# Attention with image prompts: the inputs turned by VectorE in squares of 32, the query weights in the order that this gives

## The chip, the cores and the metric

The kernel runs on one core of a Trainium2 chip. The metric is the device time of one execution in microseconds (us); the median of several executions counts. A core has five engines with a queue of instructions each: TensorE (PE in the profile; its weight loads are PEld), VectorE (DVE), ScalarE (ACT), GpSimd (POOL) and SyncE (SP). SyncE, ScalarE and GpSimd also issue DMA transfers. SBUF is the memory on the chip with 128 partitions; four quadrants of 32 partitions each play a part here. PSUM holds what TensorE writes, in eight banks.

## The reference

For a batch of 8, with 112 positions of 320 channels (`x`) and a context of 375 rows of 512 (`ctx`), of which the last 4 are image tokens, attention with 20 heads of 16 channels is computed twice, over the text and over the image tokens, and added:

```python
q = heads(x @ W_q)
k_t, v_t = heads(text @ W_k), heads(text @ W_v)          # text = ctx[:, :-4], 371 rows
probs_t = softmax(q @ k_t^T * 0.25)
text_out = probs_t @ v_t
k_ip, v_ip = heads(ip @ W_k_ip), heads(ip @ W_v_ip)      # ip = ctx[:, -4:]
qsem = l2norm(probs_t @ text)                            # 512 wide for every head and position
fused = q @ k_ip^T * 0.25 + 0.5 * (qsem @ l2norm(ip)^T)
probs_ip = softmax(fused) * spatial_mask
out = (text_out + probs_ip @ v_ip) @ W_out + b_out + x
```

## The kernel before, in words

**Steps.** The work goes in 40 steps (b, g): batch element b = 0 to 7, and group g = 0 to 4 of four heads. `qsem` is never formed. Instead the Gram matrix of a context, `ug`, is computed once for each batch element (`ps_g`, L460 for b = 0, else L498), doubled off its diagonal, with GpSimd halving the diagonal blocks (L482), and spread by SyncE's transfers to `u` (L512), four partition quadrants for the four heads of a group. The values of the text (`ps_v`, L567) go out to DRAM (L592) and come back as `vr` (L601), and GpSimd copies them beside the Gram matrix into `u` (L648). One large product for each step, `ps_qd<-u,xgT` (L730), then gives the norms of `qsem`, the text output and the products with the image tokens at a time. `xgT` are the turned probabilities of the step.

**One step.** TensorE forms the scores of four heads (`ps_s`, L682) from the keys `kT` and the queries `qm`; VectorE takes the row maxima (`nmx`, L695); ScalarE takes the exponentials (`p`, L699); SyncE moves them into four quadrants (`xg<-p`, L706); VectorE turns them in squares of 32 (`xgT`, L718); TensorE multiplies (L730); ScalarE takes the values out (`pvs`, L757) and VectorE reduces the rest (L783). Scores run two steps ahead of the product that uses them (`LEAD` = 2).

**Contexts.** The context of b = 0 is turned by TensorE against an identity matrix (`ps_c`, L430). The others are loaded in four quadrants (`load_ctx`) and turned by VectorE (`ctxT<-ct`, L418). With squares of 32, quadrant a of the result then holds channels of quadrant a of the load, so that the weights that meet this result must hold their rows in the same order; those of keys and values are loaded so.

**Queries.** Inputs are handled in five lots, `pairs` = [0], [1, 2], [3, 4], [5, 6], [7]. `x_sb` holds x by position (112 partitions), for the residual as well. `project_queries` turns a lot by identity products (`ps_x`, L332, three blocks of channels, one product for each batch element and block), each block into a PSUM bank of its own; ScalarE copies it to `xT` (L335), and nine products with `wq_sb` follow (`ps_q`, L361, and L343 for the narrow third block), whose results VectorE spreads to `qm` (L370, L353). In `xT` and `wq_sb` channel 128 i + p lies in block i, partition p; the third block is half zeros.

**What sets the order.** Nothing is scheduled by costs: the order of PE, DVE, SP, and in the steps of ACT and POOL too, is the order of the Python code, written by hand (`tc.manual_schedule`). The prologue starts everything for b = 0; then steps run in twos: `pair(n - 1)` or `alone(n)` multiplies two steps while scores of later ones are mixed in, and `behind(n)` puts the other work of a batch element (next keys `k`, values `v`, queries `q`, Gram matrix `gr`, finish `f`) behind the products. The next lot's queries are projected in `behind(n)` at even b and g = 2: its first place is the prologue (b = 0), the second b = 0, g = 2, then b = 2, 4 and 6.

**Banks.** Three pools hold the PSUM banks: `qd` (a ring of four), `sc` and `mm` (two each). `bank()` draws from the pool that the list `turn` names next; `turn` is set at the start of each `behind(n)`. A draw from a ring waits until the bank's former user has been read:

```python
elif b % 2 == 0 and g == 2:
    turn[:] = ["qd"] * 6 + ["mm"]
```

**The residual's input.** `load_inputs` (L310, GpSimd) fetches the remaining batch elements of x in three pieces, at steps n = 0 (in `behind`) and at n = 7 and 17 by the table `inputs`.

Of the kernel before, what the change touches and what calls it, by code (L numbers as in the profile page):

```python
# [8 lines left out]
F32 = mybir.dt.float32  # L9
# [11 lines left out]
def kernel(  # L21
# [81 lines left out]

    x_sb = const.tile([S, B, C], F32, tag="x_sb", name="x_sb")
    wq_sb = const.tile([P, NC, CP], F32, tag="wq_sb", name="wq_sb")
    wk_sb = const.tile([P, NE, C], F32, tag="wk_sb", name="wk_sb")
# [59 lines left out]
    ident = const.tile([P, P], F32, tag="ident", name="ident")  # L166
    make_identity(nc, ident)
    nc.gpsimd.memset(wq_sb[REST:, FULL, :], 0.0)

# [97 lines left out]
    def prompt_projections():  # L267
# [26 lines left out]
        for i in range(NC):  # L294
            nc.vector.tensor_tensor(
                kipb[:, i],
                kip[:, i, :NIP].unsqueeze(1).to_broadcast([P, HC, NIP]),
                hmask.unsqueeze(2).to_broadcast([P, HC, NIP]),
                ALU.mult,
            )  # L300
# [11 lines left out]
    queries = {}  # L312
    pairs = [[0]] + [list(range(b, min(b + 2, B))) for b in range(1, B, 2)]

    def project_queries(bs):
        n = len(bs)
        xT = work.tile([P, NC, 2 * S], F32, tag="xT", name=f"xT_{bs[0]}", bufs=1)
# [5 lines left out]
        nc.gpsimd.memset(xT[REST:, FULL, :], 0.0)  # L323
        for i in range(NC):
            cn = min(P, C - i * P)
            if bs[0] == 0:

                ps = ps_qd.tile([P, 512], F32, tag="qd", name=f"ps_x_0_{i}")
            else:
                ps = bank(f"ps_x_{bs[0]}_{i}", spare=bs[0] > 1 and i > 0)  # L330
            for j, b in enumerate(bs):
                nc.tensor.transpose(  # L332
                    ps[:cn, j * S : (j + 1) * S], x_sb[:, b, i * P : i * P + cn], ident[:S, :S]
                )
# [114 lines left out]
    def first_gram():  # L449

        ctxT = st[0]["ctxT"]
        banks = []
        for c in range(NT):
            banks.append(ps_qd.tile([P, 512], F32, tag="qd", name=f"ps_g_0_{c}"))
            if c == NT - 1:
                nc.gpsimd.tensor_copy(ctxT[:, :, TT:T], ipnT[:, :, :NIP])
            c0, c1 = c * P, min(c * P + P, T)
            for r in range(c + 1):
                for e in range(NE):
                    nc.tensor.matmul(  # L460
                        banks[r][:, c0 - r * P : c1 - r * P],
                        ctxT[:, e, r * P : (r + 1) * P],
                        ctxT[:, e, c0:c1],
                        start=(e == 0),
                        stop=(e == NE - 1),
                    )
                if c == NT - 1:
                    doubled(banks[r], r, 0)
                yield
# [585 lines left out]
    run(("q", 0), lambda: project_queries(pairs[0]), 3)  # L1055
# [3 lines left out]
    run(("q", 0), None)  # L1059
    run(("k", 0), lambda: keys(0))  # L1060
# [13 lines left out]
    placed(0, 0)  # L1074
    run(("k", 0), None, 2)
    more_constants()
    turn[:] = ["mm", "mm", "sc"]
# [52 lines left out]

    inputs = {7: (3, 5), 17: (5, B)}

    late = (1, 5)

    def pair(n):
# [40 lines left out]
        if g == 2:  # L1176
            turned(b + 2)
        value_sums(b, g)

        b, g = two  # L1180
# [32 lines left out]
    def behind(n):  # L1213
# [9 lines left out]
        if b % 2 == 0 and g == 0:  # L1223
            if n == 0:
                turn[:] = ["sc", "sc", "mm"]
            else:
                turn[:] = ["qd"] * 4 + ["mm"]
                k(b)
                nc.scalar.preload_act_table(AF.Sqrt)
                f(b - 1)  # L1230
                if b - 1 < B - 2:
                    prompt_values(b - 1)
# [13 lines left out]
            load_next(b + 2)  # L1246
            if n == 0:
                load_inputs(1, 3)
        elif b % 2 == 0 and g == 2:
            turn[:] = ["qd"] * 6 + ["mm"]  # L1250
            gram_to_groups(nb, (2,))
# [3 lines left out]
            else:  # L1255
                k(nb)
            q(nb, 3)
            tr(0)
# [55 lines left out]
        else:  # L1314
            turn[:] = ["qd"] * 3 + ["sc"]
            v(nb)
            f(b - 1)
# [9 lines left out]
    for n in range(0, len(steps) - NG, 2):  # L1327
# [145 lines left out]
```

## Time and profile before

| what | value |
| --- | --- |
| median of 3 runs | 413.02 us (412.82 to 413.89) |
| profiled execution | 412.12 us |
| its span, first to last instruction | 410.4 us |
| mean granted clock of TensorE | 0.998 |
| busy: PE, DVE, ACT, POOL | 98%, 81%, 47%, 28% of the span |
| largest shares of the chain that ended last | `ps_qd` L730 44%, `ps_v` L567 13%, `ps_k` L528 10% |

"Busy" is the time in which an engine has an instruction under way. Rows of the groups by line read: line, engine, operation, output<-input, number of instructions, then busy time and mean ns of one, then idle time before them and what ended it. Rows of a timeline read: start in us, duration in us, engine, line, operation, output<-input, number of instructions taken together, and in brackets the idle time of the engine ahead of them and what ended it. The queue that issues transfers has a q behind its engine (SPq, ACTq). The chain of waits follows the work that ended last back from instruction to instruction.

### The profile page before, as it was taken

How to read it: one execution, taken by the hardware profiler on the slowest of the kernel's cores; microseconds unless marked ns; L12 is line 12 of the kernel's file. 1: busy time of each engine (PE TensorE's matmuls, PEld its weight loads, DVE VectorE, ACT ScalarE, POOL GpSimd, SP SyncE). 2: the span in 40 equal slices, each digit the busy share in tenths (PEclk: the TensorE clock that was granted, in tenths of full speed). 3: DMA queues.
4: the chain of work that ended last, by engine and by line, in shares of the span. 5: the costliest groups of instructions: out<-in, count | busy, mean ns of one | idle time of the engine just before them, and what ended most of it. 6: DMA issues, size and time to landing. Idle time of an engine off the chain costs nothing.

```text
span 410.4 us, 14139 instructions
## 1 busy us (share of the span) xinstructions
PE 404.0 (98%) x5627; PEld 316.7 (77%) x5627; DVE 330.6 (81%) x700; ACT 194.8 (47%) x691; POOL 114.6 (28%) x271
## 2 busy tenths in 40 slices
PE   8999999999999999999999999999999999999996
PEld 8868687798777786878687877778777878687894
DVE  4356589877998887887999897887799997878985
ACT  3254342336443942524553664334733485346763
POOL 5103111121261352021161036002034125103681
PEclk9999999999999999999999999999999999999999
DMA  7777956988595746577666576576756444766311
GB/s 237 164 199 220 187 155 174 203 194 178 135 187 129 183 121 178 134 174 176 170 147 146 145 179 157 155 180 139 176 151 155 117 124 123 187 157 174 111 51 30
DMA packets 58245, 64.65 MB, mean 158 GB/s; under 512 B 19061, under 2 KB 52041, under 8 KB 58180
## 3 DMA queue, kind: packets, MB, share of 16 engines
q1 hardware_dynamic: 55230, 59.50, 59.4%
q10 hardware_dynamic: 2486, 2.69, 2.1%
q0 software_dynamic: 464, 1.56, 1.7%
q8 instruction: 45, 0.74, 0.8%
q14 instruction: 20, 0.16, 0.1%
HBM read 19.03 MB, written 5.22 MB: 59 GB/s over the span
## 4 chain that ended last, share of the span: by engine, by line
PE 93%; DMA 3%; POOL 2%; DVE 1%; ACT 0%; SPq 0%; issue 0%; POOLq 0%
PE ps_qd L730 44%; PE ps_v L567 13%; PE ps_k L528 10%; PE ps_g L498 7%; PE ps_s L682 7%; PE ps_o L886 3%; PE ps_k L545 3%; PE ps_q L361 3%; DMA u<-ug 2%; PE ps_g L460 1%; DMA xg<-p 1%; PE ps_w L447 1%; PE ps_c L430 1%; PE ps_q L343 1%; PE ps_o L982 0%; PE ps_a L877 0%
## 5 line engine op out<-in xcount | busy, mean ns | idle before, releaser
L730 PE MATMUL ps_qd<-u,xgT 32*112 32x40 f32 (+11 forms) x3840 | 215.8, 351 | 0.5 <-POOL u L648 0.4
L730 PEld LDWEIGHTS ps_qd<-u,xgT 32*112 32x112 f32 x3840 | 176.8, 172 | 36.1 <-issue 6.3
L718 DVE STREAM_TRANSPOSE xgT<-xg 128x768 f32<-128x768 f32 (+1 forms) x63 | 123.0, 1972 | 4.1 <-DMA xg<-p 3.9
L699 ACT ACTIVATE p<-ps_s,nmx 112x371 f32<-112x371 f32 x160 | 85.7, 586 | 58.2 <-DVE nmx L695 57.2
L695 DVE TENSOR_REDUCE nmx<-ps_s 112x1 f32<-112x371 f32 x160 | 77.1, 536 | 35.7 <-PE ps_s L682 33.7
L783 DVE CUSTOM_DVE_ANT_0 p<-ps_qd,p 112x371 f32<-112x371 f32 x152 | 73.5, 540 | 13.0 <-ACT pvs L757 8.3
L648 POOL COPY u<-vr 128x64 f32<-128x64 f32 x120 | 27.0, 237 | 199.0 <-PE ps_qd L730 116.4
L682 PE MATMUL ps_s<-kT,qm 32*112 32x375 f32 (+1 forms) x320 | 61.5, 485 | 0.0
L567 PE MATMUL ps_v<-wv_sb,ctxT 128*128 128x320 f32 x192 | 56.1, 439 | 0.3 <-ACT kT L535 0.3
L757 ACT COPY pvs<-ps_qd 112x21 f32<-112x21 f32 x152 | 21.9, 200 | 56.1 <-DVE ss L783 50.4
L567 PEld LDWEIGHTS ps_v<-wv_sb,ctxT 128*128 128x128 f32 x192 | 35.3, 190 | 14.6 <-ACT kT L535 1.0
L528 PE MATMUL ps_k<-ctxT,wk_sb 128*128 128x371 f32 x128 | 43.5, 483 | 0.0
L528 PEld LDWEIGHTS ps_k<-ctxT,wk_sb 128*128 128x128 f32 x128 | 23.1, 190 | 13.4 <-issue 1.3
L498 PE MATMUL ps_g<-ctxT 128*32 128x119 f32 (+11 forms) x672 | 32.4, 338 | 0.0
L498 PEld LDWEIGHTS ps_g<-ctxT 128*32 128x32 f32 x672 | 27.6, 109 | 6.0 <-issue 2.5
L682 PEld LDWEIGHTS ps_s<-kT,qm 32*112 32x112 f32 x320 | 27.7, 171 | 5.4 <-ACT p L699 0.4
L418 DVE STREAM_TRANSPOSE ctxT<-ct 128x512 f32<-128x512 f32 x21 | 22.5, 1082 | 6.0 <-DMA ct<-in_ctx_dram 6.0
L574 ACT COPY vext<-ps_v 128x320 f32<-128x320 f32 x24 | 10.2, 426 | 34.1 <-PE ps_v L567 25.5
L701 ACT COPY ipl<-ps_s 112x4 f32<-112x4 f32 x140 | 24.4, 174 | 0.0
L482 POOL TENSOR_TENSOR ug<-ug,half 128x128 f32<-128x128 f32 (+1 forms) x24 | 10.5, 447 | 32.9 <-ACT ug L481 28.1
L535 ACT COPY kT<-ps_k 128x371 f32<-128x371 f32 x16 | 7.5, 469 | 23.1 <-PE ps_k L528 22.8
L865 POOL TENSOR_TENSOR wv<-vip,w 112x1280 f32<-112x1280 f32 (+1 forms) x8 | 17.5, 2182 | 0.2 <-DVE w L859 0.2
(151 smaller groups left out, 317.6 us busy)
## 6 DMA issues: line engine op xcount, KB each, us to landing
xg<-p SPq DMA_DIRECT2D x159, 162.3 KB
u<-ug SPq DMA_DIRECT2D x128, 99.0 KB
ct<-in_ctx_dram SPq DMA_DIRECT2D x28, 176.0 KB
vip<-vipd SPq DMA_DIRECT2D x7, 560.0 KB
vr<-vd SPq DMA_DIRECT2D x20, 120.0 KB
out_dram<-ob SPq DMA_DIRECT2D x7, 140.0 KB
vd<-vext ACTq DMA_DIRECT2D x12, 80.0 KB
vr<-vd SPq DMA_DIRECT2D x12, 80.0 KB
```

Of the source, the lines that this page charges most:

```text
L418: nc.vector.transpose(ctxT[:, :, c * P : (c + 1) * P].rearrange("p e (j i) -> p j e i", i=RG), ct[:, some, :].rearrange("p j (k e) -> p j ...
L498: nc.tensor.matmul(ps[p * RG : (p + 1) * RG, s0 : T - t0], ctxT[:, e, t0 + q * RG : t0 + (q + 1) * RG], ctxT[:, e, t0 + s0 : T], start=(e ...
L528: nc.tensor.matmul(ps[:, :TT], wk_sb[:, e, i * P : (i + 1) * P], s["ctxT"][:, e, :TT], start=(e == 0), stop=(e == NE - 1),)
L567: nc.tensor.matmul(ps[:, :C], ctxT[:, e, c * P : (c + 1) * P], wv_sb[:, e, :], start=(e == 0), stop=(e == NE - 1),)
L648: nc.gpsimd.tensor_copy(region(b, c)[:, :, UV - c * P :], s["vr"][:, c * QN : (c + 1) * QN, g, :])
L682: nc.tensor.matmul(ps[:S, :w], qm[a * RG : (a + 1) * RG, i, r, j * S : (j + 1) * S], s["kT"][a * RG : (a + 1) * RG, i, :w], start=True, st ...
L695: nc.vector.tensor_reduce(nmx, ps[:S, :TT], AX.X, ALU.max, negate=True)
L699: nc.scalar.activation(p, ps[:S, :TT], AF.Exp, bias=nmx)
L701: nc.scalar.copy(s["ipl"][:, groups[g][a], :], ps[:S, TT:T])
L718: nc.vector.transpose(xT[:, j : j + n].rearrange("p j (k q) -> p q j k", q=QN), xg[:, :, j * RG : (j + n) * RG].rearrange("p q (j k) -> p ...
L730: nc.tensor.matmul(banks[a][:S, j * RG : UW], xT[a * RG : (a + 1) * RG, j, :S], region(b, c)[a * RG : (a + 1) * RG, p, q * RG :], start=(j ...
L783: nc.vector.tensor_tensor_reduce(out=p, in0=ps[:S, :TT], in1=p, scale=1.0, scalar=0.0, op0=ALU.mult, op1=ALU.add, accum_out=s["ss"][:, h : ...
```

## The change

x is loaded a second time in another form: `x_in` has 128 partitions, and quadrant q holds channels 80 q to 80 q + 79 of blocks of 32 positions, padded with zeros to 96. VectorE turns it in squares of 32 (`turned_inputs`, L353 of the changed kernel) straight to `xT`. Block i, quadrant q of `xT` then holds channels 80 q + 32 i onwards, so that `wq_sb` is loaded in that order: eight loads by GpSimd (L194, L198 of the changed kernel) in place of two by SyncE. The identity products L332, the copies L335 and the memsets L323 go. The product of a lot with its weights is as before. In `turn`, six draws from `qd` become three. The three small products of `kipb` (L295) go from VectorE to GpSimd. The residual's loads move to other steps, with batch element 0 among them.

```diff
-    nc.sync.dma_start(x_sb[:, 0, :], x[0])
-    load_channels(nc.sync, wq_sb, w_q)
...
+    def load_turned(eng, bs):
+        t0, n = blocks_of(bs)
+        rows = x.rearrange("b s c -> (b s) c")[t0 : t0 + n * RG, :]
+        for q in range(QN):
+            eng.dma_start(
+                x_in[q * RG : (q + 1) * RG, :n, :XW],
+                rows[:, q * XW : (q + 1) * XW].rearrange("(j i) c -> i j c", i=RG),
+            )
...
+    load_turned(nc.sync, pairs[0])
     load_embed(nc.sync, wk_sb, w_k)
     loaded[1] = load_ctx(1)
...
+    def load_query_weights(eng, quadrants):
+        for q in quadrants:
+            w = w_q[q * XW : (q + 1) * XW, :]
+            own = slice(q * RG, (q + 1) * RG)
+            eng.dma_start(
+                wq_sb[own, :FULL, :C], w[: FULL * RG, :].rearrange("(i c) f -> c i f", c=RG)
+            )
+            last = XW - FULL * RG
+            eng.dma_start(wq_sb[q * RG : q * RG + last, FULL, :C], w[FULL * RG :, :])
...
-            nc.vector.tensor_tensor(
+            nc.gpsimd.tensor_tensor(
                 kipb[:, i],
...
+    def turned_inputs(bs, i0=0, i1=NC):
...
+        nc.vector.transpose(
+            xT[:, i0:i1, : n * RG].rearrange("p i (j r) -> p j i r", r=RG),
+            x_in[:, :n, i0 * RG : i1 * RG].rearrange("p j (i c) -> p j i c", c=RG),
+        )
...
-        for i in range(NC):
-            cn = min(P, C - i * P)
-            if bs[0] == 0:
-                ps = ps_qd.tile([P, 512], F32, tag="qd", name=f"ps_x_0_{i}")
-            else:
-                ps = bank(f"ps_x_{bs[0]}_{i}", spare=bs[0] > 1 and i > 0)
-            for j, b in enumerate(bs):
-                nc.tensor.transpose(
-                    ps[:cn, j * S : (j + 1) * S], x_sb[:, b, i * P : i * P + cn], ident[:S, :S]
-                )
-            nc.scalar.copy(xT[:cn, i, : n * S], ps[:cn, : n * S])
-            yield
...
             if c == NT - 1:                                   # first_gram
                 nc.gpsimd.tensor_copy(ctxT[:, :, TT:T], ipnT[:, :, :NIP])
+                load_query_weights(nc.gpsimd, range(1, QN))
...
     awake(3)                                                  # prologue
+    load_query_weights(nc.gpsimd, range(1))
...
     order_values()
+    turned_inputs(pairs[0])
...
     placed(0, 0)
     run(("k", 0), None, 2)
+    load_turned(nc.gpsimd, pairs[1])
...
-    inputs = {7: (3, 5), 17: (5, B)}
+    inputs = {5: (0, 2), 9: (2, 5), 19: (5, B)}
...
         value_sums(b, g)                                      # pair
+        if b % 2 == 0 and b > 0 and g == 1:
+            turned_inputs(pairs[b // 2 + 1], 0, FULL)
...
                 turn[:] = ["sc", "sc", "mm"]                  # behind, n == 0
+                turned_inputs(pairs[1])
...
-            turn[:] = ["qd"] * 6 + ["mm"]
+            turn[:] = ["qd"] * 3 + ["mm"]
...
-            q(nb, 3)
             tr(0)
             v(nb)
             q(nb)
...
             turn[:] = ["qd"] * 3 + ["sc"]                     # behind, odd b, g == 3
+            load_turned(nc.gpsimd, pairs[(b + 3) // 2])
...
+        if b % 2 == 0 and b > 0 and g == 2:                   # main loop
+            turned_inputs(pairs[b // 2 + 1], FULL, NC)
         if n < len(steps) - NG - 1:
             value_sums(b, g)
             reduced(b, g)
```

**TensorE at the second place (b = 0, g = 2).** `ps_qd` are the last products of step (0, 2), `ps_v` the values of b = 1, `ps_q` its queries. The order before:

```order
L730 MATMUL ps_qd_2_1_704<-u_167,xgT_2_666 112x40
L290 MATMUL ps_kipT<-ident,kv 128x32 x3
L332 MATMUL ps_x_0_832<-ident,x_sb 128x112 x2
L332 MATMUL ps_x_1_836<-ident,x_sb 128x112 x2
L332 MATMUL ps_x_2_840<-ident,x_sb 64x112 x2
L567 MATMUL ps_v_1_846<-wv_sb,ctxT_246 128x320 x4
L361 MATMUL ps_q_0_852<-xT_829,wq_sb 128x224 x3
L567 MATMUL ps_v_2_862<-wv_sb,ctxT_246 128x320 x4
L730 MATMUL ps_qd_3_0_874<-u_167,xgT_3_844 112x392
```

And with the change:

```order
L761 MATMUL ps_qd_2_1_711<-u_170,xgT_2_673 112x40
L320 MATMUL ps_kipT<-ident,kv 128x32 x3
L598 MATMUL ps_v_1_838<-wv_sb,ctxT_259 128x320 x4
L391 MATMUL ps_q_0_845<-xT_589,wq_sb 128x224 x3
L598 MATMUL ps_v_2_855<-wv_sb,ctxT_259 128x320 x4
L761 MATMUL ps_qd_3_0_867<-u_170,xgT_3_836 112x392
```

The three rows of `ps_x` are gone, and the value product stands right behind the prompt's keys; the rest keeps its order.

**VectorE at the third place (b = 2).** `p_1` and `ss` are the reductions of step (2, 1), `nmx_4` the row maxima of step (2, 4), `p_2` the reductions of step (2, 2). The order before:

```order
L783 ISA ss_985 112x1
L695 TENSOR_REDUCE nmx_4_2_2142<-ps_s_2_2138 112x1
L695 TENSOR_REDUCE nmx_4_3_2148<-ps_s_3_2140 112x1
L695 TENSOR_REDUCE nmx_4_0_2169<-ps_s_0_2165 112x1
L695 TENSOR_REDUCE nmx_4_1_2174<-ps_s_1_2167 112x1
L783 ISA p_2_1822,ss_985<-ps_qd_2_0_2082,p_2_1822 112x371
```

And with the change:

```order
L814 ISA ss_978 112x1
L353 STREAM_TRANSPOSE xT_2120<-x_in 128x7x2x32
L726 TENSOR_REDUCE nmx_4_2_2142<-ps_s_2_2138 112x1
L726 TENSOR_REDUCE nmx_4_3_2148<-ps_s_3_2140 112x1
L726 TENSOR_REDUCE nmx_4_0_2169<-ps_s_0_2165 112x1
L726 TENSOR_REDUCE nmx_4_1_2174<-ps_s_1_2167 112x1
L353 STREAM_TRANSPOSE xT_2120<-x_in 128x224
L814 ISA p_2_1820,ss_978<-ps_qd_2_0_2080,p_2_1820 112x371
```

The lot is turned in two parts, 448 columns ahead of the four row maxima and 224 behind them, ahead of the next reductions.

**GpSimd in the prologue.** `ug` are the halvings of the first Gram matrix, `u` the values put beside it. The order before:

```order
L456 COPY ctxT_163<-ipnT 128x4x4
L482 TENSOR_TENSOR ug<-ug,half 128x128 x2
L482 TENSOR_TENSOR ug<-ug,half 128x115
L406 COPY ctxT_246<-ipnT 128x4x4
L323 MEMSET xT_278 64x224
L1058 COPY wq_sb<-wq_sb 128x3x64
L648 COPY u_167<-vr_168 128x4x16 x3
```

And with the change, from the last two of the eight loads of the query weights on:

```order
L194 DMA wq_sb<-in_L_xattn_W_q_dram 32x2x320
L198 DMA wq_sb<-in_L_xattn_W_q_dram 16x320
L513 TENSOR_TENSOR ug<-ug,half 128x128 x2
L513 TENSOR_TENSOR ug<-ug,half 128x115
L436 COPY ctxT_259<-ipnT 128x4x4
L1090 COPY wq_sb<-wq_sb 128x3x64
L679 COPY u_170<-vr_171 128x4x16 x3
L175 DMA x_in<-in_x_dram 32x7x80 x4
```

Two of the eight loads stand ahead of the copy of `ipnT` (L456 before) and six behind it, ahead of the halvings; four loads of the second lot of x stand behind the values.

More of the change, by code (lines that the diff above doesn't have):

```diff
@@ L104 @@
     x_sb = const.tile([S, B, C], F32, tag="x_sb", name="x_sb")
+    XW = C // QN
+    x_in = const.tile([P, 2 * S // RG, NC * RG], F32, tag="x_in", name="x_in")
     wq_sb = const.tile([P, NC, CP], F32, tag="wq_sb", name="wq_sb")
@@ L312 @@
     queries = {}
-    pairs = [[0]] + [list(range(b, min(b + 2, B))) for b in range(1, B, 2)]
+    inputs_turned = {}
+    def turned_inputs(bs, i0=0, i1=NC):
+        t0, n = blocks_of(bs)
+        if bs[0] not in inputs_turned:
+            inputs_turned[bs[0]] = work.tile(
+                [P, NC, 2 * S], F32, tag="xT", name=f"xT_{bs[0]}", bufs=1
+            )
+        xT = inputs_turned[bs[0]]
+        nc.vector.transpose(
+            xT[:, i0:i1, : n * RG].rearrange("p i (j r) -> p j i r", r=RG),
+            x_in[:, :n, i0 * RG : i1 * RG].rearrange("p j (i c) -> p j i c", c=RG),
+        )
     def project_queries(bs):
         n = len(bs)
-        xT = work.tile([P, NC, 2 * S], F32, tag="xT", name=f"xT_{bs[0]}", bufs=1)
+        at = bs[0] * S - blocks_of(bs)[0]
+        xT = inputs_turned.pop(bs[0])[:, :, at : at + n * S]
         qm = work.tile([P, NC, 2, 2 * S], F32, tag="qm", name=f"qm_{bs[0]}", bufs=2)
@@ L1058 @@
     nc.gpsimd.tensor_copy(wq_sb[:, :, C:], wq_sb[:, :, FULL * P : C])
-    run(("q", 0), None)
+    run(("q", 0), lambda: project_queries(pairs[0]))
     run(("k", 0), lambda: keys(0))
```

15 lines of the change are left out of this document (8 added, 7 removed).

## The prediction

> **What bounds the kernel now.** I read the page first, then the chain of waits, then the timeline of TensorE at the places where the change takes rows away, and last the timelines of VectorE, GpSimd and SyncE at the places where it puts rows in.
>
> From the page (span, busy time by engine, shares of the chain that ended last):
>
> ```profile
> span 410.4 us, 14139 instructions
> PE 404.0 (98%) x5627; PEld 316.7 (77%) x5627; DVE 330.6 (81%) x700; ACT 194.8 (47%) x691; POOL 114.6 (28%) x271
> PE 93%; DMA 3%; POOL 2%; DVE 1%; ACT 0%; SPq 0%; issue 0%; POOLq 0%
> ```
>
> TensorE is busy 98% of the span and is 93% of the chain: what leaves its queue leaves the time, unless what it waits for next is not ready earlier. VectorE, which receives the work, is busy 81%, so it has room only in definite gaps.
>
> **What TensorE loses.** All 24 turning products (L332) go, in five places. From the groups by line:
>
> ```profile
> L332 PE MATMUL ps_x<-ident,x_sb 112*128 112x112 f32 (+1 forms) x24 | 3.5, 264 | 0.1
> ```
>
> The 3.5 us are busy time, with neighbours overlapping. What a place costs is read between the start of its first turning product and the start of the value product behind it. From the chain of waits (start, us), the first and the fourth place, and from the timeline of TensorE the second, third and fifth:
>
> ```profile
> 15.88 0.29 PE ps_x L332 x3
> ...
> 252.94 0.58 PE ps_x L332 x6
> ```
>
> The other three:
>
> ```profile
> 59.02 1.21 PE L332 MATMUL ps_x<-ident,x_sb 112*128 112x112 f32 x6
> 60.29 2.42 PE L567 MATMUL ps_v<-wv_sb,ctxT 128*128 128x320 f32 x8
> ```
>
> ```profile
> 155.97 0.74 PE L332 MATMUL ps_x<-ident,x_sb 112*128 112x112 f32 x6
> 156.69 0.54 PE L567 MATMUL ps_v<-wv_sb,ctxT 128*128 128x320 f32 x1
> ```
>
> ```profile
> 349.58 0.45 PE L332 MATMUL ps_x<-ident,x_sb 112*128 112x112 f32 x3
> 350.30 0.54 PE L567 MATMUL ps_v<-wv_sb,ctxT 128*128 128x320 f32 x1 [0.27 <-ACT kT L535]
> ```
>
> Start to start that is 60.29 - 59.02 = 1.27, 156.69 - 155.97 = 0.72 and 350.30 - 349.58 = 0.72 us. Six products in a row are only 0.58 us of chain (the row at 252.94), so the rest of these gaps is a wait, and the change takes that away too. With six banks drawn from a ring of four, the value product gets the bank of the first draw and waits until ScalarE has emptied it. From the timeline of ScalarE:
>
> ```profile
> 59.94 0.29 ACT L293 COPY kip<-ps_kipT 128x96 f32<-128x96 f32 x1
> ```
>
> This ends at 60.23, 0.06 us before the value products start; in the last place the wait stands in the row at 350.30 itself, for a copy of ScalarE again (L535). After the change three banks are drawn, and the value product gets the second, which a score of the step before has left. The fourth place is built as the third, so I take 0.72 there as well (0.58 is the lower end). The sum on TensorE is 0.29 + 1.27 + 3 x 0.72 = 3.7 us; with the chain's 0.58, 0.58 and 0.53 (the copy in place of the products) for the last three it is 3.3.
>
> **What is late next at the second place.** The products behind it need the turned probabilities of their step (L718), on VectorE behind the three small products of L295. From the timelines of VectorE and TensorE:
>
> ```profile
> 61.76 0.39 DVE L295 TENSOR_TENSOR kipb<-kip,hmask 128x32 f32<-128x32 f32 x3
> 62.06 2.98 DVE L718 STREAM_TRANSPOSE xgT<-xg 128x1536 f32<-128x1536 f32 x1
> ```
>
> ```profile
> 65.93 0.60 PE L730 MATMUL ps_qd<-u,xgT 32*112 32x392 f32 x4
> ```
>
> TensorE would arrive at 65.93 - 1.27 = 64.66. L295 goes to GpSimd, so the turning starts at 61.76 and ends at 64.74: the step loses 0.1 us of its gain. On GpSimd the three products fall behind this row:
>
> ```profile
> 60.55 0.28 POOL L323 MEMSET xT<- 64x224 f32 x1
> 69.30 0.24 POOL L648 COPY u<-vr 128x64 f32<-128x64 f32 x1 [8.47 <-PE ps_qd L730]
> ```
>
> and the nearest product of two tensors on that engine is, in the groups,
>
> ```profile
> L482 POOL TENSOR_TENSOR ug<-ug,half 128x128 f32<-128x128 f32 (+1 forms) x24 | 10.5, 447 | 32.9 <-ACT ug L481 28.1
> ```
>
> No row shows them there. Three rows of 0.24 us (128 x 64, above) to 0.45 (L482, 128 x 128, below) would be 0.7 to 1.4 us of an idle 8.47, in which the memset L323 goes too: nothing, at both ends. They are first read by the prompt's logits, two steps later.
>
> **What VectorE gets.** Eight turnings, of 384 columns (the first place), 672 (second), 448 and 224 (third and fourth, each), 256 and 128 (fifth). Their price and the gaps they fall into, from the groups by form and the timeline of VectorE:
>
> ```profile
> L718 DVE STREAM_TRANSPOSE xgT<-xg 128x768 f32<-128x768 f32 x46 | 71.8, 1584 | 4.0 <-DMA xg<-p 3.9
> ```
>
> ```profile
> L418 DVE STREAM_TRANSPOSE ctxT<-ct 128x512 f32<-128x512 f32 x21 | 22.5, 1082 | 6.0 <-DMA ct<-in_ctx_dram 6.0
> ```
>
> ```profile
> 16.92 3.08 DVE L418 STREAM_TRANSPOSE ctxT<-ct 128x512 f32<-128x512 f32 x3 [6.00 <-DMA ct<-in_ctx_dram]
> ```
>
> ```profile
> 49.41 1.94 DVE L695 TENSOR_REDUCE nmx<-ps_s 112x1 f32<-112x371 f32 x4 [4.78 <-PE ps_s L682]
> ```
>
> ```profile
> 151.59 2.12 DVE L695 TENSOR_REDUCE nmx<-ps_s 112x1 f32<-112x371 f32 x4 [1.11 <-PE ps_s L682]
> ```
>
> ```profile
> 154.55 0.54 DVE L783 CUSTOM_DVE_ANT_0 p<-ps_qd,p 112x371 f32<-112x371 f32 x1 [0.84 <-ACT pvs L757]
> ```
>
> 1584 / 768 = 2.06 and 1082 / 512 = 2.11 ns a column; I take 2.11, since L418 has the same pattern of squares. So 0.81 us into a wait of 6.00, 1.42 into 4.78, 0.95 into 1.11, 0.47 into 0.84 (both twice), and 0.54 and 0.27 into the same two gaps of the last place. Together 5.9 us, all under cover by these rows, with 0.16 us to spare in the tightest; a gain is excluded, since VectorE only gets more to do. I cost them at nothing; uncovered, each costs what sticks out of its gap, on the way from the row maximum to the exponential and the transfer of the probabilities.
>
> **What the queues get.** SyncE issues four loads of x instead of three rows (x, and two of the query weights): one issue more, in a stretch where VectorE waits 6 us for the context. GpSimd now issues the query weights, eight loads, two before its copy at 8.49 and six behind it, ahead of the halving L482; then four loads of x for the second place ahead of more constants. The residual loads (L310) move: the one at 48.92 goes, the rest come later, with the first batch element added. From the view of that line, the timelines of GpSimd, SyncE and TensorE:
>
> ```profile
> L310 POOL DMA_DIRECT2D x_sb<-in_x_dram x3: 739/750/849, 48.9 to 208.4; - x3
> ```
>
> ```profile
> DMA to landing us min/median/max: 4.4/5.1/6.7
> ```
>
> ```profile
> 8.49 0.20 POOL L456 COPY ctxT<-ipnT 128x16 f32<-128x16 f32 x1 [2.51 <-DVE ipnT L262]
> 12.53 0.45 POOL L482 TENSOR_TENSOR ug<-ug,half 128x128 f32<-128x128 f32 x1 [3.84 <-ACT ug L477]
> ```
>
> ```profile
> 15.34 8.18 SPq L512 DMA_DIRECT2D u<-ug  x12
> ```
>
> ```profile
> 20.32 0.82 PE L361 MATMUL ps_q<-xT,wq_sb 128*128 128x112 f32 x6
> ```
>
> Six issues at 0.75 to 0.85 us from 8.69 on end at 13.2 to 13.8, so L482 starts 0.7 to 1.3 us later and its three rows end by 15.8 at worst, 0.5 us after SyncE asks for them at 15.34; those transfers are followed by ones that wait for the values anyway. The last weights are issued at 12.4 to 12.9 and land 4.4 to 6.7 us later, at 16.8 to 19.6; the first query product would now start at 20.32 - 0.29 = 20.03. So nothing is paid, with 0.4 us to spare at the far end.
>
> Here a rule of the skill speaks against the change. The Trainium skill, "SBUF — State Buffer", section "SBUF: two separate sides", says that GpSimd cannot write the descriptors of a load it issues while VectorE runs a copy in its two-port mode, and that the load should go to SyncE or ScalarE instead; the section behind it gives 3.1 us in place of 0.62 for one such load. The row that it would meet is this one, beside the second group of weight issues:
>
> ```profile
> 9.88 0.77 DVE L229 COPY wv_sb<-wv_in 128x512 f32<-128x512 f32 x2 [0.97 <-DMA wv_in<-in_L_xattn_W_v_dram]
> ```
>
> The rows of GpSimd above show no load issued beside these copies, so no run here shows it yet. If an issue waits out the 0.77 us of copies, the last weights come 0.8 us later, at 17.6 to 20.4, and TensorE waits at most 0.4 us. That is the second rival below, worked out from rows; by the skill's own figure the one load would be 2.5 us later and the sum 1 to 2 us smaller, an estimate from that page.
>
> At 86 us TensorE already waits for a transfer. From the timelines of GpSimd, TensorE and SyncE:
>
> ```profile
> 85.83 0.59 POOL L648 COPY u<-vr 128x64 f32<-128x64 f32 x3 [6.60 <-DMA xg<-p]
> ```
>
> ```profile
> 86.12 0.66 PE L730 MATMUL ps_qd<-u,xgT 32*112 32x392 f32 x3 [0.41 <-POOL u L648]
> ```
>
> ```profile
> 61.90 6.69 SPq L512 DMA_DIRECT2D u<-ug  x8
> ```
>
> ```profile
> 101.00 5.03 SPq L512 DMA_DIRECT2D u<-ug  x8
> ```
>
> If SyncE's chain of transfers before it did not move, the first two gains would end there. But the eight issues at 61.90 take 1.66 us longer than the eight at 101.00: I read the difference as a wait for the transfers of the values, which ScalarE issues when the value product is done; the trace does not name it. The value product moves 1.3 us earlier, so I expect the chain to move with it. The price of this wait lies between 0 (all moves) and 0.29 + 1.27 = 1.6 us (nothing moves); I take 0.3, near the lower end, by the 1.66 us that the row at 61.90 has over the one at 101.00.
>
> **The sum.** 3.7 - 0.1 - 0.3 = 3.3 us. The profiled execution took 412.12 us (410.4 of span and 1.7 around it), so 408.8 under the profiler; the median of the three runs is 413.02, 0.9 above, and with the same gain becomes 409.7.
>
> **The rivals.** (1) VectorE becomes the bound (slower). It is 81% busy, and two of the gaps are 1.11 us for 0.95: from 2.5 ns a column on (1.11 us over 448) the turnings stick out and delay the row maxima, the exponentials and the probabilities' transfers behind them. If all 5.9 us of them less the 0.39 of L295 came on the path, the time would be 413.0 - 3.6 + 5.5 = 414.9 (3.6 is the sum without the 0.1 of the second place). Against it stand 67 turnings in the two rows at 2.06 to 2.11 ns and the four waits quoted. The Trainium skill, "VectorE: DVE Perf Modes", section "Rules for kernel authors", advises TensorE for turning a 128 x 128 block where PSUM will do as the target; by that rule this rival would be the likelier one, and the waits quoted speak against it. Chance 0.10. (2) The query weights are late: at the far ends of issue and landing, with the copies waited out, the first query product waits 0.4 us, and twice that if the late halving also holds the first transfers: 3.3 - 0.8 = 2.5 saved, 410.5. Chance 0.10. (3) The transfers before 86 us don't move: 0.29 and 1.27 are lost in a longer wait there and 3 x 0.72 = 2.2 stays, 410.9; for it speaks that SyncE's eight issues from 61.90 on take 6.69 us already. Chance 0.17. (4) The change does nothing in the sum, (2) and (3) together with small waits in VectorE's gaps: 413.0. Chance 0.06. The forecast has the remaining 0.57; its own range is 2.8 us saved (3.3 by the chain, less 0.1 and the 0.4 of a doubled wait at 86) to 4.1 (3.7, and the 0.41 at 86 gone).
>
> **How the numbers follow.** No change here means within 0.3%, 1.24 us, about what a measurement of this kernel can tell: 411.8 to 414.3. Forecast, (2) and (3) are faster, 0.84, of which I leave 0.03 to each of the other two for sums of small waits not seen: faster 0.78, same 0.09 (rival 4 and these), slower 0.13 (rival 1 and these). The low end is 4.1 us saved and the 0.2 by which the quickest of the three runs, 412.82, lies under their median: 408.7. The high end is 412.0, halfway between (3) and (4), which leaves out (1), (4) and little else.
>
> **What would show it.** In the profile after, the value products at 15.7, 57.5, 154 and 251 us should follow their forerunners without the gap, the eight new turnings should be 2.1 ns a column with nmx (L695) starting as soon as before after its scores, and the wait at 86 should stay near 0.4 us. Wrong would be: a wait of TensorE for wq_sb near 20, a wait of 1.5 us or more where 86.12 was, or row maxima that start later behind their scores than before.

## The result, and the profile after

The changed kernel takes 411.23 us (median of 6 runs, 410.17 to 411.83) against 412.92 for the kernel before (6 runs): a ratio of 0.9959, 95% interval 0.9944 to 0.9974. It is faster, clear of the noise but by less than half a per cent: 1.7 us where 3.3 were forecast. The profiled execution took 411.26 us, 0.9 less than that of before.

The page after (span, busy time by engine, shares of the chain):

```profile
span 409.5 us, 14124 instructions
PE 402.0 (98%) x5603; PEld 316.1 (77%) x5603; DVE 333.5 (81%) x705; ACT 191.4 (47%) x676; POOL 127.6 (31%) x294
PE 92%; DMA 3%; SPq 2%; POOL 1%; ACT 1%; issue 0%; DVE 0%; POOLq 0%
```

TensorE is still the bound and has lost 2.0 us of work (404.0 to 402.0), but SyncE's queue is now on the chain with 2%. TensorE's timeline at the first, second and third place, first after, and then the one row of before that was not shown:

```profile
13.55 6.63 PE L598 MATMUL ps_v<-wv_sb,ctxT 128*128 128x320 f32 x24
```

```profile
61.12 0.35 PE L320 MATMUL ps_kipT<-ident,kv 32*128 32x32 f32 x3
61.40 2.42 PE L598 MATMUL ps_v<-wv_sb,ctxT 128*128 128x320 f32 x8
```

```profile
154.60 2.76 PE L559 MATMUL ps_k<-ctxT,wk_sb 128*128 128x371 f32 x8
157.20 2.05 PE L598 MATMUL ps_v<-wv_sb,ctxT 128*128 128x320 f32 x7
```

```profile
153.37 2.76 PE L528 MATMUL ps_k<-ctxT,wk_sb 128*128 128x371 f32 x8
```

The value products now follow their forerunners without a gap. From keys to values the third place takes 157.20 - 154.60 = 2.60 us; before it took 156.69 - 153.37 = 3.32. What was lost stands in the prologue. The waits of TensorE after:

```profile
PE ps_qd L761 <- POOL u L679: 1.1, 1, 1.1
PE ps_kv L304 <- DMA wip<-in_L_xattn_W_v_ip_dram: 0.4, 1, 0.4
```

TensorE's timeline there, before:

```profile
36.40 1.22 PE L730 MATMUL ps_qd<-u,xgT 32*112 32x392 f32 x10
...
41.76 2.42 PE L567 MATMUL ps_v<-wv_sb,ctxT 128*128 128x320 f32 x8
44.02 2.66 PE L528 MATMUL ps_k<-ctxT,wk_sb 128*128 128x371 f32 x8
46.60 1.29 PE L274 MATMUL ps_kv<-wip,ipT 128*32 128x160 f32 x32
47.83 1.22 PE L730 MATMUL ps_qd<-u,xgT 32*112 32x392 f32 x10
```

And after:

```profile
31.52 4.65 PE L529 MATMUL ps_g<-ctxT 128*32 128x375 f32 x96
37.25 0.93 PE L761 MATMUL ps_qd<-u,xgT 32*112 32x392 f32 x8 [1.08 <-POOL u L679]
...
48.16 0.47 PE L304 MATMUL ps_kv<-wip,ipT 128*32 128x160 f32 x4
49.04 1.28 PE L304 MATMUL ps_kv<-wip,ipT 128*32 128x160 f32 x28 [0.42 <-DMA wip<-in_L_xattn_W_v_ip_dram]
50.25 1.22 PE L761 MATMUL ps_qd<-u,xgT 32*112 32x392 f32 x10
```

The first big product waits for GpSimd's copies into `u`, and these wait for SyncE's transfers. GpSimd before, then after:

```profile
34.49 0.59 POOL L648 COPY u<-vr 128x64 f32<-128x64 f32 x3 [13.49 <-DMA u<-ug]
```

```profile
36.95 0.59 POOL L679 COPY u<-vr 128x64 f32<-128x64 f32 x3 [15.72 <-DMA u<-ug]
```

The same instruction's start, after less before, gives the account of the profiled execution:

| up to | before, us | after, us | after less before | what happened since the row above |
| --- | --- | --- | --- | --- |
| first query product | 20.32 | 20.02 | -0.30 | first place gained |
| first big product | 36.40 | 37.25 | +0.85 | 1.15 lost, a wait for `u` |
| values of b = 1, first part | 41.76 | 43.31 | +1.55 | 0.70 lost behind that wait |
| second big product | 47.83 | 50.25 | +2.42 | 0.87 lost, the prompt's weights |
| prompt's keys turned | 58.74 | 61.12 | +2.38 | |
| values, second place | 60.29 | 61.40 | +1.11 | 1.27 gained |
| big product of step (0, 3) | 65.93 | 67.23 | +1.30 | 0.19 lost |
| queries' third block | 76.62 | 78.40 | +1.78 | 0.48 lost |
| big product at 86 | 86.12 | 87.41 | +1.29 | 0.49 gained, the wait is gone |
| end | 410.4 | 409.5 | -0.9 | 2.19 gained, three places |

Of the 0.70 us behind the wait, 0.44 are a weight load that waits for ScalarE's copy of the next Gram matrix (`ug`, L508), which itself had waited 4.2 us for the same transfers of `u`. Of the 0.48 us behind step (0, 3), 0.21 are a weight load that waits for VectorE's spreading of the queries (`qm`, L400).

### The profile page after: what moved, and what is told of

The parts are those of the page before. It is cut to its first block, busy times and chain, and to the rows that moved or that the text cites. A ratio compares the mean times of both kernels' runs of the same rounds, so it can differ in the third digit from the quotient of the medians.

```text
span 409.5 us, 14124 instructions
## 1 busy us (share of the span) xinstructions
PE 402.0 (98%) x5603; PEld 316.1 (77%) x5603; DVE 333.5 (81%) x705; ACT 191.4 (47%) x676; POOL 127.6 (31%) x294
## 4 chain that ended last, share of the span: by engine, by line
PE 92%; DMA 3%; SPq 2%; POOL 1%; ACT 1%; issue 0%; DVE 0%; POOLq 0%
PE ps_qd L761 44%; PE ps_v L598 12%; PE ps_k L559 10%; PE ps_g L529 7%; PE ps_s L713 6%; PE ps_q L391 3%; PE ps_o L917 3%; DMA wip<-in_L_xattn_W_v_ip_dram 3%; PE ps_k L576 2%; PE ps_g L491 1%; SPq L737 1%; PE ps_w L477 1%; PE ps_c L460 1%; SPq L543 1%; PE ps_q L373 1%; PE ps_o L1013 0%
## 5 line engine op out<-in xcount | busy, mean ns | idle before, releaser
L761 PE MATMUL ps_qd<-u,xgT 32*112 32x136 f32 (+11 forms) x3840 | 216.4, 352 | 1.5 <-POOL u L679 1.1
L713 PE MATMUL ps_s<-kT,qm 32*112 32x375 f32 (+1 forms) x320 | 62.6, 485 | 0.0
```

The lines of the kernel that those rows point to most:

```text
L713: nc.tensor.matmul(ps[:S, :w], qm[a * RG : (a + 1) * RG, i, r, j * S : (j + 1) * S], s["kT"][a * RG : (a + 1) * RG, i, :w], start=True, st ...
L761: nc.tensor.matmul(banks[a][:S, j * RG : UW], xT[a * RG : (a + 1) * RG, j, :S], region(b, c)[a * RG : (a + 1) * RG, p, q * RG :], start=(j ...
```

## Experiments

The questions were why SyncE was late in the prologue, what the lateness cost, and whether VectorE's new work costs anything. In the built program every transfer of SyncE and ScalarE is dealt one of eight completion counters in turn, and waits for the transfer before it on that counter. In the changed kernel the values' way to DRAM (`vd`, ScalarE) gets counter 6 after the third of the twelve transfers of `u`, so the eleventh waits for the values:

```
ScalarE: L611 DMA vd_169<-vext_284 128x3x320 [waits DMAHW6_49,Activation_49]
SyncE:   L543 DMA u_170<-ug 32x792 [waits DMAHW5_49]
SyncE:   L543 DMA u_170<-ug 32x792 [waits DMAHW6_49]
SyncE:   L543 DMA u_170<-ug 32x792 [waits DMAHW7_49]
SyncE:   L632 DMA vr_171<-vd_169 32x12x80 [waits DMAHW0_49]
```

The trace agrees: `vd` has landed at 23.91, and the eleventh is issued at 23.92. In the kernel before `vd` has counter 7, after the fifth, and the first to wait for it is `vr`, which needs it anyway (landed 24.48, `vr` issued 24.49). SyncE's timeline after shows the stop between the tenth and the eleventh, and what comes behind it:

```profile
14.95 7.09 SPq L543 DMA_DIRECT2D u<-ug  x10
...
23.92 1.14 SPq L543 DMA_DIRECT2D u<-ug  x2
25.11 2.16 SPq L632 DMA_DIRECT2D vr<-vd  x4
27.36 3.70 SPq L737 DMA_DIRECT2D xg<-p  x4
31.12 2.48 SPq L543 DMA_DIRECT2D u<-ug  x4
```

The last four stood in the kernel before at:

```profile
30.24 2.50 SPq L512 DMA_DIRECT2D u<-ug  x4
```

The runs below were taken in three groups, each with runs of the kernel before beside it (medians 412.64, 412.84 and 412.82 us); every kernel has one profile.

**e1_counters: two loads of x to GpSimd.**

```diff
         for q in range(QN):
-            eng.dma_start(
+            own = nc.gpsimd if eng is nc.sync and q > 1 else eng
+            own.dma_start(
                 x_in[q * RG : (q + 1) * RG, :n, :XW],
```

> Changed kernel, but two of the four loads of the first lot of x (quadrants 2 and 3) are issued by GpSimd instead of SyncE, so that the transfer of the values to DRAM is dealt its completion counter after the fifth transfer of the Gram matrix instead of after the third, and no transfer of the Gram matrix waits for the values. Theory (the lost gain sits in the prologue, where SyncE's twelve transfers take 10.12 us instead of 8.18 and TensorE waits 1.08 us for u at 37): the twelve take 8.2 us again, the wait at 37 goes, and the time falls by 1.0 to 1.9 us from 411.2, to 409.3 to 410.2. Rival (it is contention on the DMA engines by the query weights, not the counter): 10 us again, and a time within 0.4 us of 411.2.

408.81 us (408.77 to 408.88, 4 runs); ratio to before 0.9906, interval 0.9890 to 0.9923. It is 2.4 us faster than the changed kernel (2.1 by the two gains over before, 3.8 and 1.7), more than expected, and the best of all; `vd` is dealt its counter after the fifth transfer again. SyncE and GpSimd:

```profile
14.68 8.54 SPq L544 DMA_DIRECT2D u<-ug  x12
24.54 1.87 SPq L633 DMA_DIRECT2D vr<-vd  x4
26.51 3.69 SPq L738 DMA_DIRECT2D xg<-p  x4
30.25 2.49 SPq L544 DMA_DIRECT2D u<-ug  x4
```

```profile
34.41 0.59 POOL L680 COPY u<-vr 128x64 f32<-128x64 f32 x3 [15.53 <-DMA u<-ug]
34.98 2.40 POOL L176 DMA_DIRECT2D x_in<-in_x_dram  x4
```

Twelve transfers take 8.54 us, the last four start at 30.25 as before (30.24), and both waits of TensorE are gone. The query weights come from GpSimd here as in the changed kernel, so the rival falls. The span is 407.1, 3.3 us under that of before, which is the prediction's sum.

**e2_early_x and e4_both: the second lot of x loaded earlier.** The line `load_turned(nc.gpsimd, pairs[1])` moves from behind `placed(0, 0)` to behind GpSimd's copy of `wq_sb`; e4 has the edit of e1 too.

> Changed kernel, but GpSimd issues the four loads of the second lot of x at about 21 us, behind its copy of the query weights, instead of at 37.6 us. Theory (these loads share the DMA engines with the prompt's weights, which land 10.74 us after their issue, and TensorE waits for them at 49): the weights land 8 to 9 us after issue, the wait at 49 goes, and the time falls by 0.4 to 0.9 us, to 410.3 to 410.8; the wait at 37 stays. Rival (the weights are late only because SyncE issued them 0.8 us later): the wait at 49 stays at 0.3 us or more and the time stays within 0.3 us of 411.2, or rises where the early loads delay the values.

412.30 us (410.86 to 415.25, 12 runs); ratio 0.999, interval 0.9971 to 1.001. The wait of 0.4 us is gone from the list (the products of the prompt's weights still take 1.84 us instead of 1.29), but the wait for `u` stays at 1.3 us and the values come back 0.5 us later (SyncE issues `vr` at 25.60). The prompt's second weights land 9.7 us after their issue, above the 8 to 9 expected, though no lot of x runs beside them. The expected gain did not come; why the median is 1.1 us above the changed kernel is not settled by the one profile, whose span is 409.6.

> Both edits together: two loads of the first lot by GpSimd, and the loads of the second lot issued at about 21 us. Theory: the gains add, 1.4 to 2.8 us below 411.2, so 408.4 to 409.8, which is where the prediction's sum (3.3 us below the kernel before) had put the change. If some other cost of the changed prologue holds, it stays above 410.4.

410.50 us (408.88 to 411.64, 6 runs); ratio 0.9939, interval 0.9915 to 0.9962. The gains do not add. The loads at 19 to 22 us run beside the values on their way to DRAM, which take 4.6 us instead of the 3.7 in e1, and SyncE issues `vr` at 25.43 instead of 24.54. One thing it does show: SyncE issues the prompt's second weights at 38.49, later than in the changed kernel (38.26), TensorE comes at 48.22 as there (48.16), and it does not wait. So the 0.87 us there was not SyncE's lateness. That it was the second lot of x beside these weights is not shown: they land 10.7 us after their issue in the changed kernel, 5.9 before, 8.3 in e4_both and 9.7 in e2_early_x without that lot beside them, and 8.3 in e1_counters with it.

**e10_one_load: one load to GpSimd.** As e1, with `q == QN - 1`.

> Changed kernel with one of the four loads of the first lot (quadrant 3) issued by GpSimd: the values' transfer is dealt its counter after the fourth transfer of the Gram matrix, so only the twelfth waits for it, and not the eleventh and twelfth. Theory (the counter's wait is what makes SyncE late): the twelfth is issued at about 23.9 and SyncE reaches the transfers back at 24.5 as in e1_counters, so 408.8 to 409.2. Rival (the number of SyncE's loads of x sets the loss, 2.4 us for two): half of it, 410.0.

410.74 us (410.03 to 411.38, 5 runs); ratio 0.9951, interval 0.9937 to 0.9966. SyncE does what was expected (`vr` at 24.41), and the time does not follow. SyncE and GpSimd:

```profile
30.41 2.48 SPq L544 DMA_DIRECT2D u<-ug  x4
```

```profile
36.41 0.59 POOL L680 COPY u<-vr 128x64 f32<-128x64 f32 x3 [14.63 <-DMA u<-ug]
```

The four transfers are issued 0.17 us later than before, and the copies that wait for them come 1.9 us later. The time lies above the theory's 408.8 to 409.2 and above the rival's 410.0: neither the counter alone nor the number of loads explains that.

**e7_before_delay1, e7_before_delay2, e9_before_delay: the kernel before with these four transfers late.** In all these profiles a DMA queue of its own (q8) fetches instructions once between 33 and 36 us, before at 34.33. The runs ask whether the transfers lose by being late or by meeting this fetch. One or two loads of 256 bytes go ahead of them on SyncE:

```diff
+    for i in range(2):
+        nc.sync.dma_start(extra[i], x[0, i : i + 1, :64])
     gram_to_groups(0, (QN - 1,))
```

> The kernel before with one tiny extra load (256 bytes, never read) issued by SyncE ahead of the last four transfers of the first Gram matrix, so that these start about 0.6 us later. Rival (a late start is passed on as it is): GpSimd's copies beside u move from 34.5 to 35.1, TensorE needs them at 36.4, nothing is lost: within 0.3 us of before. Theory (the transfers of before end 0.3 us ahead of a fetch of instructions at 34.3 us that holds one DMA engine for 1.2 us; a start later than that puts the last rows behind it): the copies move by 0.6 + 1.2 to 36.3, TensorE waits about 0.5 us at 36.4, and the time rises by 0.5 to 1.3 us.

412.57 us (411.57 to 413.78, 12 runs); ratio 0.9991, interval 0.9971 to 1.0011. No loss: issue at 30.83, copies at 35.17. It is the rival's outcome; the fetch came at 34.53 here, 0.2 us later than before, and the last rows had started by 34.42.

> The same with two extra loads, about 1.2 us. Rival: copies at 35.7, still ahead of 36.4, within 0.3 us of before. Theory: copies at 36.9, TensorE waits 1.1 us, and with the 0.76 us lost behind that wait in the changed kernel the time rises by 1.1 to 1.9 us.

416.17 us (414.95 to 418.42, 12 runs); ratio 1.0078, interval 1.0050 to 1.0105. The delay was not the one intended: both extra loads went to the same place, the second waited for the first, and the two took 2.62 us. TensorE waits 2.8 us. It shows only that lateness of `u` goes into the time.

> The kernel before with two tiny extra loads (256 bytes each, to two separate places, never read) issued by SyncE ahead of the last four transfers of the first Gram matrix: 0.94 us later by the 0.47 that one such issue took. Rival (a late start is passed on as it is): GpSimd's copies move from 34.5 to 35.4, are done at 36.0, and TensorE needs them at 36.4: within 0.3 us of before. Theory (the last rows fall behind the fetch of instructions at 34.3): copies at 36.6, TensorE waits about 0.8 us, with what is lost behind that wait 0.8 to 1.6 us slower than before.

414.37 us (413.39 to 415.45, 7 runs); ratio 1.0037, interval 1.0017 to 1.0057: 1.55 us slower, as the theory expected and against the rival. The delay was 1.54 us and not 0.94: SyncE reaches `vr` at 25.30 in this profile, 0.81 later than before, ahead of anything that the edit adds. The four are issued at 31.78 and the fetch comes at 35.50, not at 34.3, so the copies start at 38.21, later than the 36.6 expected; passed on as it is, the delay would have put them at 36.0. TensorE waits:

```profile
38.50 0.93 PE L731 MATMUL ps_qd<-u,xgT 32*112 32x392 f32 x8 [1.38 <-POOL u L649]
```

Put side by side, the kernels fall into two classes with nothing between. In the traces a transfer has 16 landing records, and the copies wait for the last; the two last ones of the fourth transfer, and the time in which the fetch of instructions is under way, stand in the table:

| kernel | four transfers issued, us | copies start, us | between | 15th and 16th landing, us | fetch, us | median, us |
| --- | --- | --- | --- | --- | --- | --- |
| before | 30.24 | 34.49 | 4.25 | 34.28, 34.30 | 34.33 to 35.54 | 412.9 |
| e1_counters | 30.25 | 34.41 | 4.16 | 34.28, 34.30 | 34.07 to 35.16 | 408.8 |
| e7_before_delay1 | 30.83 | 35.17 | 4.34 | 34.86, 34.88 | 34.53 to 35.90 | 412.6 |
| e10_one_load | 30.41 | 36.41 | 6.00 | 34.47, 36.21 | 33.46 to 34.94 | 410.7 |
| changed kernel | 31.12 | 36.95 | 5.83 | 35.20, 36.67 | 34.30 to 35.42 | 411.2 |
| e4_both | 31.15 | 37.01 | 5.86 | 35.20, 36.90 | 34.20 to 35.63 | 410.5 |
| e2_early_x | 31.61 | 37.29 | 5.68 | 35.70, 37.01 | 33.94 to 35.51 | 412.3 |
| e9_before_delay | 31.78 | 38.21 | 6.43 | 35.89, 37.83 | 35.50 to 36.57 | 414.4 |

In the first three rows the two landings are 0.02 us apart, and so they are, within 0.02, in e5, e6 and e8 below. In the other five the last one is 1.3 to 1.9 us late (in e7_before_delay2 it is the first transfer's, 35.73 and 37.64).

The DMA view in slices of 1 us tells them apart (packets by size, and the queue that fetches instructions, with MB and share of 16 engines). Before, 34 to 35 and 35 to 36:

```profile
DMA packets 90, 0.15 MB, mean 147 GB/s; under 512 B 1, under 2 KB 89, under 8 KB 89
...
q8 instruction: 1, 0.02, 7.6%
```

```profile
DMA packets 126, 0.17 MB, mean 166 GB/s; under 512 B 14, under 2 KB 126, under 8 KB 126
```

After, the same slices:

```profile
DMA packets 66, 0.12 MB, mean 124 GB/s; under 512 B 31, under 2 KB 31, under 8 KB 65
...
q8 instruction: 1, 0.02, 7.0%
```

```profile
DMA packets 114, 0.16 MB, mean 159 GB/s; under 512 B 9, under 2 KB 112, under 8 KB 114
```

One packet of q8 has 7.0 to 9.2% of 16 engines for 1 us, that is one engine for 1.1 to 1.5 us. The rows of `u` have 3.1 KB and stand between "under 2 KB" and "under 8 KB". Before, none is left when the fetch comes (89 and 89). After, 34 of them are in the same slice as the fetch (65 less 31), and two more follow in the next slice (114 less 112), though the four transfers had been issued by 33.6. In e10_one_load TensorE runs 0.7 us ahead of before (Gram matrix at 31.10 instead of 31.82), the fetch stands in the slice from 33 to 34, and two rows trail in the one from 34 to 35:

```profile
DMA packets 71, 0.18 MB, mean 184 GB/s; under 512 B 17, under 2 KB 17, under 8 KB 70
...
q8 instruction: 1, 0.02, 9.2%
```

```profile
DMA packets 71, 0.09 MB, mean 88 GB/s; under 512 B 14, under 2 KB 69, under 8 KB 71
```

The late rows begin when the fetch ends: in the changed kernel at 35.40 and 35.73, where the fetch ends at 35.42; in e10 at 34.92 and 35.25, where it ends at 34.94; in the three others within 0.02 us of its end too. One landing of 16 is late, and the other 15 are not. So these rows stood behind the fetch on one engine. The collision can come about in two ways, by transfers that come later (the changed kernel, where the fetch is not earlier) and by a fetch that comes earlier (e10, 0.9 us). What sets the time of the fetch was not tried, and no run took it away. The room is small even in e1, where the last rows end at 34.01 and the fetch begins at 34.07. The Trainium skill, "DMA: Bandwidth & Descriptors", section "Queues, rings and completion order", says that each DMA engine goes round its queues a packet at a time; the late rows agree with that.

**e5_double_turning: e1 with each turning of x done twice.**

> The kernel of e1_counters (408.8 us) with every turning of x by VectorE done twice into the same place, so that VectorE has 4.3 us more work (the eight turnings took 4.3 us in the changed kernel). Theory (they lie in gaps of VectorE): 408.8 to 409.4, the 0.6 for the two gaps of 1.11 us that would now hold 1.28 us. Rival (VectorE is the bound): the whole 4.3 us come on top, 413.

408.90 us (408.44 to 411.76, 6 runs), 0.1 above e1 and so inside the theory's range; ratio to before 0.9894, interval 0.9851 to 0.9937. VectorE at the third place:

```profile
149.04 1.32 DVE L355 STREAM_TRANSPOSE xT<-x_in 128x448 f32<-128x448 f32 x2
150.28 2.04 DVE L728 TENSOR_REDUCE nmx<-ps_s 112x1 f32<-112x371 f32 x4
```

Even twice the work costs nothing that can be measured: the rival, VectorE as the bound, falls.

**e8_kipb_vector: e1 with `kipb` back on VectorE.**

> The kernel of e1_counters with the three small products of the prompt's keys (kipb) back on VectorE, ahead of the turning of the probabilities that TensorE waits for at the second place. Theory (after the change VectorE is what is late there, the chain of e1_counters goes over that turning): 0.3 us slower, 409.1. Rival: no change within 0.15 us.

409.07 us (408.83 to 410.56, 6 runs), 0.26 above e1, near the expected 0.3, but the runs spread by more. VectorE, then TensorE:

```profile
61.80 0.39 DVE L326 TENSOR_TENSOR kipb<-kip,hmask 128x32 f32<-128x32 f32 x3
62.11 2.94 DVE L750 STREAM_TRANSPOSE xgT<-xg 128x1536 f32<-128x1536 f32 x1
```

```profile
65.19 1.22 PE L762 MATMUL ps_qd<-u,xgT 32*112 32x392 f32 x9 [0.42 <-DVE xgT L750]
```

In the profile it is plainer. From the value product on, the big product comes after 65.19 - 59.06 = 6.13 us here and after 64.63 - 58.78 = 5.85 in e1. The turned probabilities are what is late next at the second place, as predicted.

**e6_before_banks: the kernel before with another order of banks.**

```diff
-            turn[:] = ["qd"] * 6 + ["mm"]
+            turn[:] = ["qd"] * 4 + ["mm"] + ["qd"] * 2
```

> The kernel before, its turning products kept, with one edit: the list of banks for the places after even batch elements draws the first value product from mm instead of the ring of four, and the second from the ring. Theory (part of the 1.27 and 0.72 us of a place is a wait for a bank): the value product follows the turning products at once, 0.6 us after their start, so 0.65 + 3 x 0.14 = about 1.1 us less than before, 411.8 from 412.9. Rival (the products alone cost that time, or the bank of mm is not free there either): within 0.3 us of before.

414.48 us (413.80 to 415.12, 6 runs); ratio 1.0044, interval 1.0027 to 1.0060: slower. Two of its places on TensorE:

```profile
59.64 1.21 PE L332 MATMUL ps_x<-ident,x_sb 112*128 112x112 f32 x6
61.12 2.42 PE L567 MATMUL ps_v<-wv_sb,ctxT 128*128 128x320 f32 x8 [0.27 <-DVE ss L783]
```

```profile
156.82 0.74 PE L332 MATMUL ps_x<-ident,x_sb 112*128 112x112 f32 x6
157.40 2.33 PE L567 MATMUL ps_v<-wv_sb,ctxT 128*128 128x320 f32 x8
```

At the third place the products alone take 0.58 us, so 0.14 of the 0.72 was the bank. The fourth and the fifth place go the same way, 254.54 - 253.96 = 0.58 and 351.39 - 351.11 = 0.28 us instead of 0.72. At the second the wait only changes its releaser (1.48 us instead of 1.27). That the kernel is slower all the same is neither the theory's outcome nor the rival's. Its second place begins 0.62 us later than before (59.64 instead of 59.02), ahead of all that the edit touches; where the rest went is not settled.

## Why the prediction was right or wrong

The measured 411.23 us lies in the forecast's range of 408.7 to 412.0, and the time moved the way that was forecast. That is in part luck: the gain is half of the forecast one, the range was wide enough to hold rival (3) as well, and what was lost was lost where the prediction had put nothing.

**Right: what TensorE loses.** Forecast 3.7 us; measured 0.30 + 1.27 + 2.19 = 3.76 by the account above (from keys to values 0.72, 0.72 and 0.71 less at the last three places). The bank as the reason for part of the gap is borne out at those three places by e6.

**Right in sign, wrong in price: VectorE's turnings.** They cost nothing, as forecast, and with much more room: they took 4.3 us in all and not 5.9, and e5 doubles them for 0.1 us. Rival (1) falls, and here the Trainium skill's advice for TensorE ("VectorE: DVE Perf Modes", section "Rules for kernel authors") would have kept the slower kernel: TensorE is the engine at 98%, and its turning products cost 3.76 us.

**Right: the query weights.** The first query product starts at 20.02 without a wait, and the halving behind the issues starts at 12.53, as before and not 0.7 to 1.3 us later. The overlap of a GpSimd load with VectorE's copies, of which the Trainium skill warns, shows at one issue and is small: the one at 9.16 took 0.73 us, where the three others of its line (L198) took 0.51 to 0.53, and it ended at 9.89, 0.10 us after the first of VectorE's copies of `wv_sb` (9.37 to 9.79). The next, at 9.88, beside the rest of these copies (to 10.46), took 0.54 us, as did those at 8.63 and 10.90. So 0.2 us of delay, not 0.77, and nothing waited for it. The eight loads landed 6.0 to 7.9 us after their issue, above the 4.4 to 6.7 I had taken, but were issued sooner (by 11.9). Rival (2) falls.

**Wrong: "So nothing is paid".** This is the step that failed. I priced SyncE's one more issue and GpSimd's loads by their own time and asked whether the engine that issues them has room. Not priced were the counter that `vd` is dealt, which moves when the issues before it do (SyncE reaches `vr` 0.6 us later and the four transfers 0.9), the fetch behind it (copies another 1.6 us later), and the prompt's second weights, which land 10.7 us after their issue instead of 5.9; why they do is open. The account shows 1.15 + 0.70 + 0.87 = 2.7 us lost. The same kind of wait stood in the prediction's own row at 61.90: the fifth of those eight transfers is issued at 66.17, when a transfer of the values on its counter has landed (66.15). It was read there as a wait for the values, and not looked for in the prologue. e1, which lets all of the 2.7 us go, has the 3.3 us of the sum in its span; two wrong terms cancel in that, since the wait at 86 gives 0.48 us there where 0.3 was charged, and 0.47 goes behind the second place where nothing was. How the 2.7 divides between the counter and the fetch is not fixed: with the counter nearly out of play, e10 is still 1.9 us behind e1.

**Wrong in size and sign: the wait at 86.** I charged 0.3 us for transfers that do not move; TensorE does not wait there at all after, a gain of 0.49. Rival (3) gave almost the measured time, 410.9, and is wrong all the same: the loss lies before 50 us.

**Too small: what is late at the second place.** 0.19 us instead of 0.1, and another 0.48 in the products behind it (0.47 in e1). VectorE's spreading of the queries accounts for 0.21 of that; the rest no run explains.

## What to carry to other kernels

A transfer is priced by what it is queued behind and what it runs beside, not by its issue time: where a change adds or moves one, look in the built program at which completion counter each of the next transfers waits for, and beside what each lands. Work taken off the bounding engine is a safe gain only if the transfers that feed it keep their margin: here 0.9 us of lateness put two rows of 3.1 KB behind a fetch of instructions and made the copies 2.5 us late. Before giving up a change that gave half of what it should, restore which transfer waits for which: here moving two loads from SyncE to GpSimd put the values' transfer back behind the fifth, and the gain over before went from 1.7 to 3.8 us. Moving one, which gave SyncE its old number of loads, did not.

## What the hardware showed that I had not expected

VectorE's turning has two prices. For x it is the lower one; the groups by form after:

```profile
L749 DVE STREAM_TRANSPOSE xgT<-xg 128x768 f32<-128x768 f32 x46 | 71.6, 1581 | 5.3 <-DMA xg<-p 5.1
L749 DVE STREAM_TRANSPOSE xgT<-xg 128x1536 f32<-128x1536 f32 x17 | 51.5, 3028 | 0.1
...
L353 DVE STREAM_TRANSPOSE xT<-x_in 128x672 f32<-128x672 f32 x1 | 0.9, 878 | 3.5 <-DMA x_in<-in_x_dram 3.5
...
L353 DVE STREAM_TRANSPOSE xT<-x_in 128x128 f32<-128x128 f32 x1 | 0.3, 299 | 0.0
```

That is (878 - 299) / 544 = 1.06 ns a column and 0.16 us for each instruction. The probabilities take (3028 - 1581) / 768 = 1.88 ns a column by the same difference. What the difference hangs on was not tried. And a fetch of instructions of 1.1 to 1.6 us on one of 16 DMA engines makes the copies 1.5 to 2 us later: one landing of 16 is late, and the copies start 0.1 to 0.4 us after it.
